# A gated recurrent layer: weights loaded by quarters of 32 rows, and two small moves inside a step

## The chip, the cores and the metric

The kernel runs on one core of a Trainium2 chip. The metric is the device time of one execution in microseconds (us); before the change it is 1395.19 us, the median of three runs (1394.82 to 1395.47). Every engine of the core has its own instruction queue and runs it in order: TensorE (PE; its weight loads are shown apart as PEld), VectorE (DVE), ScalarE (ACT), GpSimd (POOL) and SyncE (SP). SyncE only issues DMAs here; ScalarE and GpSimd issue a few as well.

## The reference

The input x has 64 sequences of 128 steps with 512 values each, h starts from `cond_1024`, and the result is x plus the states of a gated recurrent layer, all in float32:

```python
def step(h, inp):
    x_t, prop = inp
    comb = jnp.concatenate([x_t, h], axis=-1)
    z = jax.nn.sigmoid(comb @ Wz + bz)
    r = jax.nn.sigmoid(comb @ Wr + br)
    comb2 = jnp.concatenate([x_t, r * h], axis=-1)
    h_cand = jnp.tanh(comb2 @ Wh + bh)
    h_new = (1.0 - z) * h + z * h_cand
    h_next = jnp.where(prop, jnp.tanh(h_new @ Wp + bp), h_new)
    return (h_next, h_new)
```

Every fourth step is a prop step, in which a projection follows (31 of the 128). Wz, Wr and Wh are 1024 x 512: the upper 512 rows meet x, the lower 512 meet h. Wp is 512 x 512.

## The kernel before

**Layout.** A matrix of 512 x 512 lies in SBUF as `[128, K = 4, 512]`: four chunks k of 128 rows. The partitions are four quarters q of 32 (`part(q)`), and partition 32q + e of chunk k holds row q*128 + k*32 + e. The three upper halves lie in one tile `wx`, the lower halves in `wh[R]`, `wh[Z]`, `wh[H_]`, the projection in `wp`. A state h lies as 128 partitions x 256 values, in two halves `s_` of 128.

**The part that depends on x** is worked out ahead. For steps 0 to 3 and the last two by plain products (`plain`, `plain_last`), for all the others by a scheme of seven products instead of eight, for which sums of weight blocks are formed in place in `wx` (`sum_outer_1`, `sum_inner_1`). Chunks 0, 1 and 2 of `wx` are changed by that, chunk 3 isn't. All these products are units in a `queue`, and `fill(n)` puts n of them into TensorE's order at fixed places of a step: a list `PLACES` for the steady steps, `HEAD` and `TAIL` for the first and last ones. The results, with biases, become the seeds that `seed` copies into PSUM before a gate adds its part.

**A step** (the loop at L611) is, in program order: gate R on TensorE (16 matmul calls, 32 instructions); sigmoid of r, r*h and its transpose by halves; the seed of R for the next step; gate Z, its sigmoid, `keep` = (z - 1)*h; the seed of Z; in a prop step a copy of the projection's bias `bias_p` into PSUM (L695); `places[0]` units; gate H; its tanh by halves, each multiplied by z; one subtraction of `keep` over both halves (L727); the transpose to `hT`; the seed of H; `places[1]` units; in a prop step the projection with its tanh and transpose, and `places[2]` units. GpSimd adds h to x in `xr`, and SyncE stores four steps at a time.

**The start.** SyncE issues, in this order: half of the first x (ScalarE issues the other half), 12 DMAs for `wx` (R, Z, H; four chunks each), 4 for `wh[R]`, 8 for the next part of x, 4 for `wh[Z]`, 4 for `wh[H_]`, then x for steps 4 to 7 (`xr_1`) and 8 to 11 (`xs_2`), 4 for `wp` and 4 for `bias_p`. GpSimd issues the bias rows, waits for chunk 1 of R (`held`, L119) and then issues h0. TensorE runs 112 matmuls over zeros (`idle`) and then works in a fixed order: the x products of steps 0 and 1 for R, the spreading of the bias rows, the same products for Z and H, then step 0, in which 12 units stand between gate Z and gate H.

**The end.** In step T - 7 `reload` (L427) fetches chunks 2, 0 and 1 of `wx` again, since the last two steps use the plain weights. `plain_last` has the products of chunk 3 first, then chunks 2, 0, 1 for step T - 2, gate by gate, and then those of step T - 1. The SyncE queue then loads the last `xr`.

Of the kernel before, what the change touches and what calls it, by code (L numbers as in the profile page):

```python
# [18 lines left out]
def kernel(  # L19
# [14 lines left out]
    nc = tc.nc  # L34
    B, T, D = x.shape
    H = h0.shape[1]
    P = 128
    S = 2
    V = B // S
    NQ = P // V  # L40
    J = H // NQ
    C = 2
    K = D // P
# [4 lines left out]
    R, Z, H_ = range(3)  # L48
# [22 lines left out]
    wx = const.tile([P, K, 3, H], F32, name="wx")  # L71
    wh = [const.tile([P, K, H], F32, name=f"wh_{i}") for i in range(3)]
    wp = const.tile([P, K, H], F32, name="wp")
# [3 lines left out]
    gates_in = (Wr, Wz, Wh)  # L77
# [5 lines left out]
    def part(q):  # L83
        return slice(q * V, (q + 1) * V)

    def load_x(tile_, t0, n, j=0, engs=(nc.sync,)):
        i = 0
        for h in range(S):
            for q in range(NQ):
                engs[i % len(engs)].dma_start(  # L90
                    out=tile_[part(q), j : j + n, h, :], in_=x[ts(h, V), t0 : t0 + n, ts(q, J)]
                )
                i += 1

    def load_w(wt, w, k, eng=nc.sync):
        eng.dma_start(
            out=wt[:, k, :],
            in_=w.rearrange("(q k e) n -> k q e n", q=NQ, k=K)[k],
        )

    xr = {}

# [5 lines left out]
    bias_p = const.tile([P, S, J], F32, name="bias_p")  # L108
    new_xr(0)
    load_x(xr[0], 0, 2, engs=(nc.sync, nc.scalar))  # L110
    for i in range(3):
        for k in range(K):
            load_w(wx[:, :, i, :], gates_in[i][:D], k)

    for i, b in enumerate((br, bh, bz)):
        nc.gpsimd.dma_start(out=bias_row[:, i, :], in_=b.rearrange("(o n) -> o n", o=1))
# [3 lines left out]
    for h in range(S):  # L120
        nc.gpsimd.dma_start(
            out=h_init[:, h, :],
            in_=h0[ts(h, V), :].rearrange("b (q j) -> q b j", q=NQ),
        )
    for i in range(3):
        for k in range(K):
            load_w(wh[i], gates_in[i][D:], k)
        if i == 0:
            load_x(xr[0], 2, 2, 2)

# [5 lines left out]
    def load_xs(g):  # L136
        if g * Q4 < T:
            xs[g] = one.tile([P, Q4, S, J], F32, tag=f"xs{g % 2}", name=f"xs_{g}")
            load_x(xs[g], g * Q4, Q4)
# [1 line left out]
    new_xr(1)  # L141
    load_x(xr[1], Q4, Q4)
    load_xs(2)
    for k in range(K):
        load_w(wp, Wp, k)
    for q in range(NQ):
        nc.sync.dma_start(
            out=bias_p[part(q)],
            in_=bp.rearrange("(o d c j) -> c o d j", o=1, d=2, c=2)[q % 2].broadcast_to(
                [V, S, J]  # L150
            ),
# [3 lines left out]
    P_ = 3  # L155
    r, z = rec[H_][:, 1], rec[Z][:, 1]

    def gate_ps(i):
        return rec[0][:, 1] if i == P_ else rec[i][:, 0]
# [66 lines left out]
    def crossed(dst, h, ps, func):  # L226
        for d in range(2):
            nc.scalar.activation(  # L228
                dst[ts(d, 2 * V), h, :], ps[ts(h, 2 * V), d, :], func
            )  # L230

    def turn(dst, src):
        nc.vector.transpose(out=dst, in_=src)  # L233
# [134 lines left out]
    def seed(i, t):  # L368
        if t < T:
            nc.scalar.copy(  # L370
                gate_ps(i).rearrange("p d (c n) -> p d c n", c=C),
                G[t][:, :, :, i, :].rearrange("p c d n -> p d c n"),
            )
# [51 lines left out]
        return seq  # L425

    def reload():  # L427
        for k in (2, 0, 1):
            for i in range(3):
                load_w(wx[:, :, i, :], gates_in[i][:D], k)  # L430

    MB = {}

# [177 lines left out]
    for t in range(T):  # L611
        g, j = divmod(t, Q4)
        prop = j == CHUNK - 1 and t < T - 1
# [60 lines left out]
            turn(rhT[:, s_, :], rh[:, s_, :])  # L674
        if t != 3:
            seed(R, t + 1)
        if last:
            seed(H_, t)
        join(0)
# [2 lines left out]
        keep = two.tile([P, S, J], F32, tag="keep", name=f"keep_{t}")  # L682
        for s_ in range(S):
            crossed(z, s_, gate_ps(Z), AF.Sigmoid)
        nc.vector.scalar_tensor_tensor(  # L685
            out=keep, in0=z, scalar=1.0, in1=h, op0=ALU.subtract, op1=ALU.mult
# [4 lines left out]
        if t == 3:  # L691
            seed(R, t + 1)
        seed(Z, t + 1)
        if prop:
            nc.scalar.copy(gate_ps(P_), bias_p)  # L695
        if last:
            nc.gpsimd.tensor_sub(xr[g][:, j], xr[g][:, j], keep)
        if t == 0:
# [8 lines left out]
        if t == T - 7:  # L707
            reload()

        gate(H_, rhT, wh[H_])  # L710
        h_new = two.tile([P, S, J], F32, tag="h", name=f"h_{t}")
        hT = None if last else new_T("hT", f"hT_{t}")
        cand = two.tile([P, S, J], F32, tag="c", name=f"c_{t}")
        for s_ in range(S):
            crossed(cand, s_, gate_ps(H_), AF.Tanh)
            c = z[:, s_, :]
            nc.vector.tensor_mul(c, cand[:, s_, :], c)  # L717
            if last:
                o = xr[g][:, j, s_, :]
                nc.vector.tensor_add(o, c, o)  # L720
                (nc.sync, nc.scalar)[s_].dma_start(
                    out=out[ts(s_, V), t, :].rearrange("b (q n) -> q b n", q=NQ),
                    in_=o,
                )
                continue
        if not last:
            nc.vector.tensor_sub(h_new, z, keep)  # L727
            turn(hT, h_new)
        if t < T - 2:
            seed(H_, t + 1)  # L730
# [64 lines left out]
        n = 0  # L795
        if t >= T - CHUNK:
            n = 3 if t == T - 2 else 0
        elif j == Q4 - 1:
            n = 4
        if n:  # L800
            for s_ in range(S):
                for q in range(NQ):
                    nc.sync.dma_start(
                        out=out[ts(s_, V), t - n + 1 : t + 1, ts(q, J)],
                        in_=xr[g][part(q), j - n + 1 : j + 1, s_, :],
# [50 lines left out]
```

## Time and profile before

| | |
|---|---|
| median of the runs | 1395.19 us |
| profiled execution | 1394.77 us |
| its span, first to last instruction | 1392.7 us |
| mean granted clock of TensorE | 0.983 |
| TensorE matmul busy | 1324.7 us (95%) |
| VectorE busy | 733.7 us (53%) |
| ScalarE busy | 728.3 us (52%) |
| GpSimd busy | 887.4 us (64%) |
| TensorE busy, 0 to 128 us | 96.1 us |
| TensorE busy, 128 to 1320 us | 1170.5 of 1192 us |
| TensorE busy, 1320 to 1392.7 us | 58.1 us |

A page of the profile gives each engine's busy time, its busy share in 40 slices of the span (a digit is tenths, 9 is 90% or more), the clock that TensorE was granted (PEclk, tenths of full speed) and the mean busy share of the core's 16 DMA engines. A timeline row is: start, duration, engine, line, operation, output<-input, shapes, count, and in brackets how long the engine had been idle before and what released it. L202 is the matmul helper of all gates and units; the tile names tell them apart. L228 is the activation helper, L370 the seed, L717 the product with z. SPq, ACTq and PEq are an engine's queue: a DMA row there is the issue of the DMA, not its transfer.

### The profile page before, as it was taken

To read this page: it belongs to the slowest core of one execution; us is meant where nothing else is said; L and a number is where in the kernel's file an instruction comes from. 1 tells how busy PE (TensorE), PEld (TensorE's weight loads), DVE (VectorE), ACT (ScalarE), POOL (GpSimd) and SP (SyncE) were. 2 spreads that over 40 slices of the span, in tenths; PEclk is the share of its full clock that TensorE was granted. 3 is DMA by queue.
4 is the path that set the end of the run, shared out by engine and by line. 5 is a ranking of instruction groups with operands and counts; after the bars stand their busy time and mean duration, and the time that the engine had idled before them with its cause. 6 is when DMAs were issued, how large, how long until landed. Compare 5 with 4: busy or idle time off the path is not lost. (4 is left out here: it accounts for less than half of the span.)

```text
span 1392.7 us, 59942 instructions
## 1 busy us (share of the span) xinstructions
PE 1324.7 (95%) x26024; PEld 924.6 (66%) x26024; DVE 733.7 (53%) x1909; ACT 728.3 (52%) x2401; POOL 887.4 (64%) x1030
## 2 busy tenths in 40 slices
PE   7599999999999999999999999999999999999987
PEld 2256766767676676766667677676767667676654
DVE  0254555555555555555555555555555555555533
ACT  0034555555555555555555555555555555555544
POOL 1277776767777676767757676775767667576420
PEclk7699999999999999999999999999999999999999
DMA  2330111112101111110111111011111111111030
GB/s 97 109 93 21 41 48 37 48 33 54 42 21 48 46 48 33 48 44 23 48 48 48 33 42 45 27 48 49 48 33 33 48 32 48 47 35 33 18 100 17
DMA packets 114148, 63.14 MB, mean 45 GB/s; under 512 B 12604, under 2 KB 109116, under 8 KB 113884
## 3 DMA queue, kind: packets, MB, share of 16 engines
q1 hardware_dynamic: 113176, 58.97, 15.1%
q8 instruction: 204, 3.34, 1.0%
q14 instruction: 60, 0.49, 0.1%
q10 hardware_dynamic: 452, 0.20, 0.1%
q0 software_dynamic: 256, 0.14, 0.0%
HBM read 42.47 MB, written 16.78 MB: 43 GB/s over the span
## 5 line engine op out<-in xcount | busy, mean ns | idle before, releaser
L228 ACT ACTIVATE rec_h<-rec_r 64x128 f32<-64x128 f32 x512 | 128.0, 250 | 347.7 <-PE rec_r L202 291.8
L202 PE MATMUL rec_h<-wh,rhT 128*32 128x256 f32 x4096 | 274.4, 381 | 5.4 <-DVE rh L673 3.7
L202 PEld LDWEIGHTS rec_h<-wh,rhT 128*32 128x32 f32 x4096 | 166.0, 110 | 76.7 <-DVE rh L673 24.7
L202 PE MATMUL rec_r<-wh,hT 128*32 128x256 f32 x3072 | 184.9, 381 | 12.6 <-DVE hT L233 11.6
L202 PE MATMUL rec_z<-wh,hT 128*32 128x256 f32 x3072 | 183.8, 379 | 0.0
L793 POOL TENSOR_TENSOR xr<-xr,h 128x256 f32<-128x256 f32 x127 | 93.1, 733 | 133.7 <-DVE h L727 133.7
L228 ACT ACTIVATE c<-rec_h 64x128 f32<-64x128 f32 x512 | 139.5, 272 | 71.4 <-PE rec_h L202 64.8
L527 POOL TENSOR_TENSOR cp<-mb,mb 128x768 f32<-128x768 f32 x75 | 137.1, 1828 | 42.5 <-DVE mb L496 38.9
L527 POOL TENSOR_TENSOR mb<-mb,mb 128x768 f32<-128x768 f32 x58 | 106.2, 1831 | 83.0 <-DVE mb L496 83.0
L202 PEld LDWEIGHTS rec_r<-wh,hT 128*32 128x32 f32 x3072 | 96.6, 110 | 85.2 <-DVE hT L233 24.7
L673 DVE TENSOR_TENSOR rh<-rec_h,h 128x128 f32<-128x128 f32 x192 | 56.0, 291 | 173.0 <-ACT rec_h L228 173.0
L717 DVE TENSOR_TENSOR rec_z<-c,rec_z 128x128 f32<-128x128 f32 x256 | 75.7, 296 | 131.4 <-ACT c L228 126.3
L202 PEld LDWEIGHTS rec_z<-wh,hT 128*32 128x32 f32 x3072 | 103.8, 110 | 62.0
L228 ACT ACTIVATE rec_z<-rec_z 64x128 f32<-64x128 f32 x512 | 128.0, 250 | 26.9 <-PE rec_z L202 11.8
L527 POOL TENSOR_TENSOR cp<-mb 128x768 f32<-128x768 f32 x47 | 86.1, 1832 | 60.7 <-ACT rec_h L370 59.2
L469 ACT COPY cq<-scratch_q 128x384 f32<-128x384 f32 (+1 forms) x214 | 102.4, 479 | 22.0 <-PE scratch_q L202 18.3
L532 POOL TENSOR_TENSOR mb<-mb,bias_x 128x768 f32<-128x768 f32 x35 | 64.2, 1834 | 43.9 <-DVE mb L496 43.9
L233 DVE STREAM_TRANSPOSE rhT<-rh 128x128 f32<-128x128 f32 x256 | 79.8, 312 | 8.7
L492 DVE TENSOR_TENSOR mb<-scratch_q,cx 128x384 f32<-128x384 f32 (+1 forms) x107 | 58.1, 543 | 49.1 <-ACT cq L469 49.1
L685 DVE SCALAR_TENSOR_TENSOR keep<-rec_z,h 128x256 f32<-128x256 f32 x96 | 40.8, 425 | 79.0 <-ACT rec_z L228 79.0
L370 ACT COPY rec_z<-cp 128x256 f32<-128x256 f32 x128 | 48.2, 376 | 61.9 <-DVE keep L685 61.9
L527 POOL TENSOR_TENSOR cp<-cp,mb 128x768 f32<-128x768 f32 x29 | 53.2, 1834 | 32.7 <-DVE mb L496 31.6
(157 smaller groups left out, 2817.2 us busy)
## 6 DMA issues: line engine op xcount, KB each, us to landing
out_dram<-xr SPq DMA_DIRECT2D x249, 64.0 KB
xr<-in_x_dram SPq DMA_DIRECT2D x248, 64.0 KB
xs<-in_x_dram SPq DMA_DIRECT2D x240, 64.0 KB
wx<-in_L_cond_Wr_dram SPq DMA_DIRECT2D x7, 256.0 KB
wx<-in_L_cond_Wz_dram SPq DMA_DIRECT2D x7, 256.0 KB
wx<-in_L_cond_Wh_dram SPq DMA_DIRECT2D x7, 256.0 KB
wh<-in_L_cond_Wr_dram SPq DMA_DIRECT2D x4, 256.0 KB
wh<-in_L_cond_Wz_dram SPq DMA_DIRECT2D x4, 256.0 KB
```

The lines of the kernel that those rows point to most:

```text
L202: nc.tensor.matmul(ps[part(2 * h + c)], lhsT=lhs(h), rhs=rhs(c), start=start, stop=True, skip_group_check=True,)
L228: nc.scalar.activation(dst[ts(d, 2 * V), h, :], ps[ts(h, 2 * V), d, :], func)
L233: nc.vector.transpose(out=dst, in_=src)
L370: nc.scalar.copy(gate_ps(i).rearrange("p d (c n) -> p d c n", c=C), G[t][:, :, :, i, :].rearrange("p c d n -> p d c n"),)
L469: nc.scalar.copy(c[:, :nm], ps[:, :nm])
L492: nc.vector.tensor_add(blocks(1, 1), runs(q_ps[:, :nm]), runs(T2[what][:, :nm]))
L527: nc.gpsimd.tensor_add(dst, a, b)
L532: nc.gpsimd.tensor_add(m, m, v.unsqueeze(1).to_broadcast([P, 2, 3 * J]))
L673: nc.vector.tensor_mul(rh[:, s_, :], r[:, s_, :], h[:, s_, :])
L685: nc.vector.scalar_tensor_tensor(out=keep, in0=z, scalar=1.0, in1=h, op0=ALU.subtract, op1=ALU.mult)
L717: nc.vector.tensor_mul(c, cand[:, s_, :], c)
L793: nc.gpsimd.tensor_add(xr[g][:, j], xr[g][:, j], h_new)
```

## The change

Four edits. `load_w` no longer issues one DMA for each chunk of 128 rows (source cut into q, e, n) but one for each quarter of 32 partitions, with chunks k0 to k1 in it (source cut into e, k, n), over one queue or several in turn. R's part of `wx` goes in two pairs of chunks, the quarters in turn on SyncE and ScalarE; every other matrix goes as four DMAs on SyncE. `reload` goes matrix by matrix, chunks 0 to 2 in each DMA: 12 DMAs where there were 9. The copy of `bias_p` moves from behind the seed of Z to behind the seed of R (in step 3, where that seed comes later, to the same place without it). The subtraction of `keep` goes into the loop over the halves, so that half 0 is done between the two products with z.

```diff
-    def load_w(wt, w, k, eng=nc.sync):
-        eng.dma_start(
-            out=wt[:, k, :],
-            in_=w.rearrange("(q k e) n -> k q e n", q=NQ, k=K)[k],
-        )
+    def load_w(wt, w, k0=0, k1=K, engs=(nc.sync,)):
+        for q in range(NQ):
+            engs[q % len(engs)].dma_start(
+                out=wt[part(q), k0:k1, :],
+                in_=w[q * P + k0 * V : q * P + k1 * V, :].rearrange("(k e) n -> e k n", e=V),
+            )
...
-    for i in range(3):
-        for k in range(K):
-            load_w(wx[:, :, i, :], gates_in[i][:D], k)
+    for k in range(0, K, 2):
+        load_w(wx[:, :, R, :], gates_in[R][:D], k, k + 2, (nc.sync, nc.scalar))
+    for i in (Z, H_):
+        load_w(wx[:, :, i, :], gates_in[i][:D])
...
-        for k in range(K):
-            load_w(wh[i], gates_in[i][D:], k)
+        load_w(wh[i], gates_in[i][D:])
...
-    for k in range(K):
-        load_w(wp, Wp, k)
+    load_w(wp, Wp)
...
     def reload():
-        for k in (2, 0, 1):
-            for i in range(3):
-                load_w(wx[:, :, i, :], gates_in[i][:D], k)
+        for i in range(3):
+            load_w(wx[:, :, i, :], gates_in[i][:D], 0, 3)
...
         if t != 3:
             seed(R, t + 1)
+        if prop:
+            nc.scalar.copy(gate_ps(P_), bias_p)
         if last:
             seed(H_, t)
         join(0)
...
         seed(Z, t + 1)
-        if prop:
-            nc.scalar.copy(gate_ps(P_), bias_p)
...
                 continue
+            nc.vector.tensor_sub(h_new[:, s_, :], c, keep[:, s_, :])
         if not last:
-            nc.vector.tensor_sub(h_new, z, keep)
             turn(hT, h_new)
```

## The prediction

> **What bounds the kernel now.** I read the page's slices first, then SyncE's own timeline, then the stretches, and last the instruction timeline at the places the change touches. The slices:
>
> ```profile
> PE   7599999999999999999999999999999999999987
> PEclk7699999999999999999999999999999999999999
> DMA  2330111112101111110111111011111111111030
> ```
>
> One slice is 34.8 us. From the third on TensorE is the bound: between 128 and 1320 us it is busy for 1170.5 of 1192 us. What is not bound by it is the start (two slices of low clock, high DMA share) and the end. SyncE's queue shows what the start is made of:
>
> ```profile
> 5.54 10.47 SPq L96 DMA_DIRECT2D wx<-in_L_cond_Wz_dram  x4
> 16.06 10.02 SPq L96 DMA_DIRECT2D wx<-in_L_cond_Wh_dram  x4
> ...
> 50.39 9.71 SPq L96 DMA_DIRECT2D wh<-in_L_cond_Wh_dram  x4
> ...
> 176.88 3.65 SPq L90 DMA_DIRECT2D xr<-in_x_dram  x8
> ```
>
> Four weight DMAs (1.05 MB) hold the queue for 10 us; eight loads of x (0.52 MB) issue in 3.65 us. The columns of the next view are length, five busy times, the clock, the share of 16 DMA engines and GB/s:
>
> ```profile
> 18.00:20.00 2.00, 2.00 (x16) 0.39 (x12) 0.00 (x0) 0.00 (x0) 0.00 (x0) 0.50 0.26 102
> 142.00:143.00 1.00, 0.67 (x15) 0.42 (x16) 1.00 (x3) 0.00 (x0) 1.00 (x2) 1.00 0.54 155
> 1342.00:1343.00 1.00, 1.00 (x27) 0.73 (x20) 0.00 (x0) 0.00 (x0) 0.00 (x0) 1.00 0.60 198
> ```
>
> A weight stream by chunks of 128 rows runs at 102 GB/s with a share of 0.26, which is 4.2 of 16 engines; its source is cut into q, e, n with q = 4 outermost. The loads of x go to 32 partitions with 32 rows outermost, move in smaller runs (512 B), and still reach 0.54 and 155 GB/s. The new weight DMAs have the shape of the loads of x: 32 rows outermost. I read the 0.26 as four engines at work, and expect the new DMAs to use all 16.
>
> **Weights at the start.** TensorE waits for each chunk; the last waits are those that set the end of the start:
>
> ```profile
> 60.95 0.20 PEld L202 LDWEIGHTS rec_z<-wh,hT_init 128*32 128x32 f32 x8 [2.36 <-DMA wh<-in_L_cond_Wz_dram]
> ...
> 71.82 0.16 PEld L202 LDWEIGHTS rec_h<-wh,rhT 128*32 128x32 f32 x8 [1.58 <-DMA wh<-in_L_cond_Wh_dram]
> 72.06 0.78 PEld L202 LDWEIGHTS scratch_a<-wx,xT 128*32 128x32 f32 x16
> ```
>
> After 72.06 no matmul waits for a weight DMA until the end of the kernel, so the time at which the H gate of step 0 is done is what to compare. Up to the last chunk of Wz's lower half, 5.64 MB have moved (wx 3.15, h0 0.13, x's second part 0.26, wh for R and Z 2.10). At 102 GB/s this is 55.3 us; 60.95 leaves 5.65 us for the first x, the issue and the landing, which I keep.
>
> The rate after the change lies between 102 GB/s (nothing gained) and 16 engines at what one gives now, 102 / (0.26 x 16) = 24.5, so 392. The nearest rows are the loads of x: 155, which SyncE's issue held down (64 KB in 3.65 / 8 = 0.46 us is 144 GB/s), and 198, where the tail of a weight stream and loads of x ran together. I take 198, the most that a row shows with 32-row destinations in the stream. SyncE issues an unobstructed 256 KB weight DMA in 0.55 us, so issue doesn't limit at this rate.
>
> The Trainium skill, page "SBUF — State Buffer", section "Door 1: The DMA port swizzle", speaks against this edit: bandwidth follows how many of 16 ports the partitions reach, 32 partitions reach 8, and its advice is 128 partitions for every DMA-bound transfer. It gives 189 GB/s for 32 partitions against 328 for 128. The trace has 102 for 128 partitions and 155 for 32 of them, the other way round, so the rule alone would give a loss here; its figure of 189 would make the sum below 2.0 us worse (1.4 at the start, 0.6 in the reload).
>
> At 198, Wz lands at 5.65 + 28.5 = 34.1. Then, in TensorE's order, come gate Z (32 instructions), 12 fill units (96) and gate H (32). Rates: 54 ns an instruction at full clock (32 in 1.73 us, 77.45 to 79.18), 107 ns at half. Before 34.1 TensorE idles some 5 us, so I let it start at half clock, and let it rise after 5 us of work, as it did from 61.4 to 66.2: 47 instructions in 5.0, 81 in 4.4, so 43.5; wh for H landed at 39.4; gate H 1.7, so 45.2. The same working on the old trace gives 69.2 for the end of the fill, where the timeline has 69.25. The first fill unit behind gate H moves from 72.3 to 45.2: **-27.1**. VectorE does not take the place: from the keep of step 0 it has 7.5 us of work (63.2 to 70.7: `sum_outer`, three bias adds), so it is free near 46.4 and h about 1 us late, while 12 fill units (5.2 us) cover it. GpSimd's sums come forward with the weights. With the other ends: 392 GB/s leaves TensorE as the bound from 8.87 on, 192 + 32 + 32 + 96 + 32 instructions of 54 ns plus 1.4 for the bias rows, so 31.0 (-41.2); 155 gives 42.0 and so -19.2; 102 means the four chunks of a gate are worked off together after the last (+1.3).
>
> R's halves go out on SyncE and ScalarE. ScalarE gets four DMAs of about 0.5 us in front of a table load at 2.67; its first real work is at 20.75, so this is nothing; without that cover, 2 us. The bias rows, the `held` copy and h0 behind it stay on GpSimd's queue and come no later.
>
> **The reload.** Before, it went by chunk in the order 2, 0, 1, as the last readers finished:
>
> ```profile
> 1322.94 0.58 SPq L96 DMA_DIRECT2D wx<-in_L_cond_Wr_dram  x1
> ...
> 1327.65 0.83 PE L202 MATMUL scratch_r<-wx,s12r 128*32 128x192 f32 x16
> ...
> 1341.60 1.93 PE L202 MATMUL rec_r<-wh,hT 128*32 128x256 f32 x32 [0.94 <-DVE hT L233]
> ```
>
> Now each DMA carries all three chunks, so the first must wait for the readers of chunk 1 in the row at 1327.65, some 5.3 us later, and R, Z and H come one after another. 2.36 MB at 198 GB/s are 11.9 us; with 2.4 from issue to first byte and landing (first bytes of the reload lie 1.3 after its issue; 1.1 is my estimate for the landing, from chunks that a wait released 1.1 us after the stretches count their bytes) H lands near 1342.8. R and Z are in time (readers at 1338.42 and 1338.85). The reader of H at 1339.28 isn't: it and the unit behind it end at 1343.7, and behind them gate R of the next step waits, which started at 1341.60 after 0.94 us of wait for h. **+2.1**, and the steps after it are a chain, so it stays. 155 GB/s: H at 1346.1, +5.4. 392: the issue of 12 DMAs sets it, 0. 102: +13.3. Queued behind it on SyncE is the last load of x, used 20 us later.
>
> **h in halves.** The chain of one step:
>
> ```profile
> 1339.57 0.30 DVE L717 TENSOR_TENSOR rec_z<-c,rec_z 128x128 f32<-128x128 f32 x1 [1.29 <-ACT c L228]
> 1340.15 0.30 DVE L717 TENSOR_TENSOR rec_z<-c,rec_z 128x128 f32<-128x128 f32 x1 [0.29 <-ACT c L228]
> 1340.55 0.42 DVE L727 TENSOR_TENSOR h<-rec_z,keep 128x256 f32<-128x256 f32 x1
> 1341.01 0.45 DVE L233 STREAM_TRANSPOSE hT<-h 128x256 f32<-128x256 f32 x1
> ```
>
> First product to transpose: 1.44. After: product 0.40 (start to start, 1340.15 to 1340.55), half a subtraction 0.25 to 0.33 (0.29 for such a tile at L673), product 0.40, half 0.33: 1.38 to 1.46. The first half blocks the second product for about what the smaller last one saves. Only where TensorE waits for hT (63 times, 30 us) can it gain, at most 63 x 0.07 = 4.4. Where VectorE runs late anyhow (61 products out of 254 did not wait for a tanh, so at most 30 steps), the extra instruction costs 0.18: 5.4. I take **0**. The added 127 x 0.16 = 20 us lie in VectorE's 47% of idle time.
>
> **The bias of the projection.**
>
> ```profile
> 691.71 0.37 ACT L695 COPY rec_r<-bias_p 128x256 f32<-128x256 f32 x1
> 692.10 1.14 ACT L228 ACTIVATE c<-rec_h 64x128 f32<-64x128 f32 x4
> ```
>
> The tanh starts straight behind it. In the new place, behind the seed of r, it stands before the sigmoid of z, which also follows its predecessor without a gap (689.42 + 0.38, then 689.82): sigmoid, keep and seed of z come 0.38 later, and the tanh finds the same time. **0**; bounds: -2.2 (gate H was done 0.07 before the tanh, 31 times) and +11.8 (all 31 x 0.38 on the path).
>
> **Sum.** 1394.77 (this execution; span 1392.7 and 2.1 around it) - 27.1 + 2.1 = 1369.8. The median of the runs is 0.4 above it: **1370**.
>
> **Rivals.** *More than eight ports' worth* (over 300 GB/s): TensorE bounds the start, 1395.2 - 41.2 = 1354. For it: 24.5 GB/s an engine. Against: no row is above 198. Chance 0.10. *The rate of x* (155 and less): 1395.2 - 19.2 + 5.4 = 1381. For it: the stretch at 142; against: its issue limit. 0.13. *The weights stay slow* (slower side): the 32-row DMAs give no more than 102 GB/s, each gate starts only at its last quarter, and the reload stalls the tail: 1395.2 + 1.3 + 13.3 = 1410. It decides below some 122 GB/s, where start (-9.2) and reload (+9.2) cancel. For it: 128 rows fill every partition at once, 32 rows a quarter; against: 155 with smaller runs. 0.10, and 0.03 for a rate near that balance, no change. The forecast has 0.64.
>
> Its own range is 1366 to 1374. The 8 in 10 take in most of both neighbours on the faster side: 1355 to 1384. About 0.2% (2.8 us) is what a measurement here can tell from nothing. Faster 0.87, same 0.03, slower 0.10.
>
> **What would show it.** Right: weight stretches near 200 GB/s with a share above 0.5; full clock from about 40 us; a wait of TensorE of 2 to 4 us for wx near the reload; half subtractions before the second product at no gain. Wrong: a share of 0.26 still, matmuls of gate Z waiting past 50 us, or ScalarE's sigmoid of z late enough in the prop steps that TensorE waits for h there.

## The result, and the profile after

The changed kernel takes 1372.93 us, the median of four runs (1372.32 to 1374.43), beside 1395.30 before: a ratio of 0.9842, with a 95% interval of 0.9825 to 0.9859. The forecast was 1370, in a range of 1355 to 1384. The profiled execution took 1372.32, with a span of 1370.3 against 1392.7. The slices of the changed kernel:

```profile
PEclk9999999999999999999999999999999999999999
DMA  8401112101111111112101111111111101111030
```

The clock of the first two slices, 7 and 6 tenths before, is now 9, and the DMA engines have a high share (8 tenths) in the first slice alone. SyncE's queue and two stretches of the changed kernel:

```profile
6.19 2.53 SPq L97 DMA_DIRECT2D wx<-in_L_cond_Wz_dram  x4
11.45 5.99 SPq L97 DMA_DIRECT2D wh<-in_L_cond_Wr_dram  x4
18.27 8.06 SPq L90 DMA_DIRECT2D xr<-in_x_dram  x8
26.38 1.86 SPq L97 DMA_DIRECT2D wh<-in_L_cond_Wz_dram  x4
```

```profile
18.00:20.00 2.00, 2.00 (x24) 1.15 (x20) 0.00 (x0) 0.00 (x0) 0.00 (x0) 0.50 1.06 227
24.00:26.00 2.00, 2.00 (x40) 0.96 (x31) 1.09 (x3) 0.38 (x1) 1.96 (x2) 1.00 0.30 70
```

In the first of these stretches the weight stream runs at 227 GB/s and all 16 engines are busy (1.06, with overlapping packets), where it was 102 and 0.26. The stretches of 2 us between 4 and 24 us have 172 to 266. But there is a hole: from 18.3 to 26.3 us eight loads of x of 32 KB hold SyncE, the engines run low behind them (70 GB/s), and Wz's lower half is issued only then. TensorE's timeline:

```profile
33.48 3.64 PE L202 MATMUL rec_z<-wh,hT_init 128*32 128x256 f32 x32 [5.41 <-DMA wh<-in_L_cond_Wz_dram]
...
44.19 1.05 PE L202 MATMUL scratch_a<-wx,xT 128*32 128x256 f32 x16
```

The first fill unit behind gate H of step 0 starts at 44.19, where it was 72.27: 28.1 us earlier. Only 22.4 of them are left at the end of the span. Setting the transposes of h in both traces side by side, step by step, shows where the rest goes: 28.1 us ahead in steps 1 and 2, 28.3 in step 10, 26.7 in step 37, 24.8 in step 79, 22.5 in step 121, 22.4 in step 126. It is lost evenly over the whole run, and not at random: about 0.10 in each prop step, 0.18 in each step t = 5 mod 8, next to nothing elsewhere.

### The profile page after: what moved, and what is told of

It reads as the page before. It is cut to its first block, busy times and chain, and to the rows that moved or that the text cites. A ratio compares the mean times of both kernels' runs of the same rounds, so it can differ in the third digit from the quotient of the medians.

```text
span 1370.3 us, 60091 instructions
## 1 busy us (share of the span) xinstructions
PE 1315.0 (96%) x26024; PEld 925.3 (68%) x26024; DVE 753.5 (55%) x2036; ACT 730.2 (53%) x2401; POOL 887.3 (65%) x1030
## 5 line engine op out<-in xcount | busy, mean ns | idle before, releaser
L202 PE MATMUL rec_r<-wh,hT 128*32 128x256 f32 x3072 | 184.9, 381 | 14.4 <-DVE hT L233 13.3
L725 DVE TENSOR_TENSOR h<-rec_z,keep 128x128 f32<-128x128 f32 x254 | 74.0, 292 | 16.4
```

The source lines that it names most:

```text
L202: nc.tensor.matmul(ps[part(2 * h + c)], lhsT=lhs(h), rhs=rhs(c), start=start, stop=True, skip_group_check=True,)
L725: nc.vector.tensor_sub(h_new[:, s_, :], c, keep[:, s_, :])
```

## The experiments

All times are medians; ratios are to the kernel before, run beside them on the same chip, with 95% intervals. The start itself differs from run to run: in five runs with the same loads at the start (the changed kernel and four kernels below), gate Z of step 0 began between 31.9 and 34.5 us. Differences of a microsecond or two are therefore read from the steps, not from the medians.

### What the two small moves cost

The subtraction over both halves again, the rest as changed:

```diff
-            nc.vector.tensor_sub(h_new[:, s_, :], c, keep[:, s_, :])
         if not last:
+            nc.vector.tensor_sub(h_new, z, keep)
             turn(hT, h_new)
```

> The changed kernel with the subtraction of keep over both halves again, all else as changed. Theory A (the two small moves gave back what is missing after the start): the first of every eight-step period's late steps, t = 5 mod 8, loses 0.18 us no more (15 times), so about 2.7 us faster than the changed kernel, near 1370.2. Rival B (the moves are neutral, and the 5.7 us between step 6 and the end come from a shifted meeting of stores, loads and GpSimd's sums): 1372.9.

Measured: 1368.64 us (1367.76 to 1369.49), ratio 0.9806 (0.9792 to 0.9819), 4.3 under the changed kernel. Step by step, it moves ahead of the changed kernel by 0.18 in each step t = 5 mod 8 and by 0.01 to 0.02 in most others; 3.6 us from step 4 to step 122, where theory A expected 2.7.

The bias copy behind the seed of z again, the rest as changed:

```diff
             seed(R, t + 1)
-        if prop:
-            nc.scalar.copy(gate_ps(P_), bias_p)
...
         seed(Z, t + 1)
+        if prop:
+            nc.scalar.copy(gate_ps(P_), bias_p)
```

> The changed kernel with the projection's bias copied behind the seed of z again. Theory A: each of 31 prop steps is 0.10 us shorter, so about 3.1 us faster than the changed kernel, near 1369.8. Rival B: 1372.9. Rival C (the half subtraction alone is the loss, also in the prop steps): 1372.9 here and 1367 without the halves.

Measured: 1369.69 us (1368.83 to 1370.25), ratio 0.9813 (0.9800 to 0.9826), 3.2 under the changed kernel; it gains 0.10 us in each prop step and nothing in the others, 3.1 us from step 7 to step 121.

Both undone, so that only the loads are changed:

> Only the new weight loads: subtraction and bias copy as in the kernel before. Theory A: both losses gone, about 5.8 us under the changed kernel, near 1367, 28 us under the kernel before. Rival B: 1372.9.

Measured: 1366.59 us (1366.21 to 1366.82), ratio 0.9791 (0.9778 to 0.9804). Its lead over the kernel before is 28.4 us in step 5 and 29.0 in step 122: nothing is given back on the way. Against the changed kernel it gains 6.4 us in these steps, close to the 3.6 and 3.1 of the two runs above together.

Only the two moves, with the loads of before:

> Only the half subtractions and the moved bias copy, weights loaded by chunks of 128 rows as before. Theory A: about 5.8 us slower than the kernel before, near 1401. Rival B: 1395.3, no change. If the halves saved anything by themselves: below 1395.

Measured: 1400.57 us (1400.37 to 1402.95), ratio 1.0042 (1.0028 to 1.0056); its lag behind the kernel before grows from nothing to 5.7 us with the same pattern of steps. Theory A holds in all four runs and rival B falls: it does not need the earlier start. Rival C falls with the run in which the bias alone was put back.

Why each costs is in the rows. VectorE of the kernel before, in a step t = 5 mod 8:

```profile
714.40 0.55 DVE L496 TENSOR_TENSOR mb<-scratch_y,cq 128x384 f32<-128x384 f32 x1
714.87 0.69 DVE L717 TENSOR_TENSOR rec_z<-c,rec_z 128x128 f32<-128x128 f32 x2
715.66 0.42 DVE L727 TENSOR_TENSOR h<-rec_z,keep 128x256 f32<-128x256 f32 x1
716.12 0.45 DVE L233 STREAM_TRANSPOSE hT<-h 128x256 f32<-128x256 f32 x1
```

The same step of the changed kernel:

```profile
688.99 0.28 DVE L716 TENSOR_TENSOR rec_z<-c,rec_z 128x128 f32<-128x128 f32 x1
689.38 0.29 DVE L725 TENSOR_TENSOR h<-rec_z,keep 128x128 f32<-128x128 f32 x1
689.78 0.30 DVE L716 TENSOR_TENSOR rec_z<-c,rec_z 128x128 f32<-128x128 f32 x1
690.11 0.29 DVE L725 TENSOR_TENSOR h<-rec_z,keep 128x128 f32<-128x128 f32 x1
690.43 0.45 DVE L233 STREAM_TRANSPOSE hT<-h 128x256 f32<-128x256 f32 x1
```

No row has an idle time: VectorE comes late from evacuating a batch, and both tanhs are done by then. There is nothing left to overlap with, so the fourth instruction is simply added: from the first product to the transpose it is 1.44 us where it was 1.25. In a step where VectorE does wait for a tanh, the same distance is 1.45 (1326.04 to 1327.49 in the changed kernel) where it was 1.44 (1339.57 to 1341.01): the split gains nothing there either.

ScalarE of the changed kernel, in a prop step:

```profile
663.44 0.38 ACT L370 COPY rec_r<-cp 128x256 f32<-128x256 f32 x1
663.85 0.38 ACT L677 COPY rec_r<-bias_p 128x256 f32<-128x256 f32 x1
664.25 1.09 ACT L228 ACTIVATE rec_z<-rec_z 64x128 f32<-64x128 f32 x4
665.83 0.38 ACT L370 COPY rec_z<-cp 128x256 f32<-128x256 f32 x1 [0.49 <-DVE keep L686]
666.22 1.14 ACT L228 ACTIVATE c<-rec_h 64x128 f32<-64x128 f32 x4
```

The copy stands on one chain with the tanh in either place, but its price isn't the same: behind the seed of r it starts 0.41 after it, behind the seed of z it started 0.31 after it (691.40, 691.71), and what follows comes 0.39 to 0.40 later in both. From the seed of r to the tanh it is 2.78, where it was 2.68 (689.42 to 692.10). Why the two copies stand further apart here was not tried; that both go to one PSUM tile (`rec_r`) and the seed of z to another is a guess.

### A place where the copy costs nothing

In the rows above ScalarE waits 0.49 us for the keep, between the sigmoid and the seed of z. The run with the loads only, with the copy there:

```diff
             crossed(z, s_, gate_ps(Z), AF.Sigmoid)
+        if prop:
+            nc.scalar.copy(gate_ps(P_), bias_p)
```

> Loads only, and the projection's bias copied between the sigmoid of z and the seed of Z, where ScalarE waits 0.49 us for the keep in every step. The copy takes 0.37. Theory S (the copy cost time in both places because ScalarE had no gap there; in a gap it costs nothing): the tanh of a prop step starts when gate H is done, 0.07 us earlier than with the copy behind the seed of Z, 31 times, so 2.2 us under the run with the loads only, near 1364.4. Rival (a copy into that bank costs wherever it stands): 1366.6 or more.

Measured: 1365.73 us (1363.36 to 1368.05), ratio 0.9790 (0.9777 to 0.9803). By the median it can't be told from the run with the loads only. By the steps it can: 0.08 us gained in each prop step and nothing elsewhere, 2.2 us from step 4 to step 121, on top of a profiled start that happened to be 1.7 later and a reload that cost 2.1 more (its rows follow under the reload below).

### What makes the weight loads fast

Chunks in order again, but each as four DMAs of 32 rows, 64 KB; small moves undone:

```diff
+        for k in range(k0, k1):
             for q in range(NQ):
                 engs[q % len(engs)].dma_start(
-                    out=wt[part(q), k0:k1, :],
-                    in_=w[q * P + k0 * V : q * P + k1 * V, :].rearrange("(k e) n -> e k n", e=V),
+                    out=wt[part(q), k, :],
+                    in_=w[q * P + k * V : q * P + (k + 1) * V, :],
                 )
```

> Small moves undone; weights by chunk k again, but each chunk as four DMAs of 32 rows (64 KB, one 2 KB row to a partition) instead of one of 128 rows. Theory E (the outermost count of a DMA decides how many of the 16 engines work; 32 gives all): share above 0.5 in the weight stream, and the rate is held by the issue, 64 KB in some 0.46 us or 140 GB/s; Wz's lower half lands near 45 us instead of 33.5, the reload (36 DMAs, 16 us) stalls the end some more: 1378 to 1386. Rival F (a DMA is fast because four rows go to each partition): 102 GB/s and a share of 0.26, time of the kernel before or more.

Measured: 1387.99 us (1383.65 to 1389.20), ratio 0.9943 (0.9923 to 0.9962), 2 us above the expected range. Gate Z of step 0 had its last chunk at 45.13 us, as expected; the reload cost 7.5 us. The same DMAs with the source cut with 4 outermost:

```diff
-                    in_=w[q * P + k * V : q * P + (k + 1) * V, :],
+                    in_=w[q * P + k * V : q * P + (k + 1) * V, :].rearrange("(e a) n -> a e n", a=4),
```

> As the run by chunks of 32 rows, but the source of each DMA is cut so that 4 is its outermost count (rows 0, 4, 8 ... first). The rows land in another order in their quarter, so the output isn't the reference's; bytes, DMAs, partitions and queues are the same. Theory E: four engines again, a share of 0.26 and 102 GB/s, Wz's lower half lands near 60 us, and with the reload that must wait: 1395 to 1410. Rival G (32 partitions or the quarter order is what makes it fast): the same time as the run by chunks of 32 rows.

Measured: 1412.98 us (1412.57 to 1414.34), ratio 1.0129 (1.0114 to 1.0144): 18.3 us behind the kernel before in the last steps, 3.6 to 4.4 of them from the start and 14.7 from the reload. A stretch of the weight stream in each of the two, the shorter cut first:

```profile
16.00:20.00 4.00, 2.91 (x52) 1.63 (x48) 0.75 (x2) 0.71 (x2) 0.75 (x1) 1.00 0.53 143
```

```profile
20.00:24.00 4.00, 3.76 (x32) 0.95 (x24) 0.00 (x0) 1.02 (x3) 0.99 (x1) 0.50 0.27 102
```

The first is at its issue limit (64 KB in 0.46 us is 143 GB/s), the second at four engines' pace. Bytes, number, partitions and queues of the DMAs are the same, only the outermost count of the source differs: theory E holds, F and G fall. The Trainium skill states such a rule, page "DMA: Bandwidth & Descriptors", section "Why a DMA increments its semaphore by 16 and not by 1": the number of engines is the largest number up to 16 that divides the outermost dimension of both sides. With 4 of 16 it gives a share of 0.25, where the rows have 0.26 and 0.27; with 32 it gives 16, where the changed kernel has 1.06.

Row p*4 + k in partition p, so that a matrix is one DMA with 128 partitions outermost, and the transposes read with a step:

```diff
+            out=wt[:, k0:k1, :],
+            in_=w.rearrange("(p k) n -> p k n", k=K)[:, k0:k1, :],
...
-        in_=src[:, i].rearrange("p h (k e) -> p h k e", k=K),
+        in_=src[:, i].rearrange("p h (e k) -> p h k e", k=K),
...
-        nc.vector.transpose(out=dst, in_=src)
+                in_=src.rearrange("p (e k) -> p k e", k=K),
```

> Small moves undone; row p*4 + k of a matrix in partition p, chunk k, so that each matrix is one DMA with 128 partitions outermost; the transposes of x, h and r*h read their rows with a step of 4 to match. Theory P: over 300 GB/s, the start bound by TensorE, 1352 to 1360 if a transpose with a step costs what it cost (0.31, 0.45 us). If the step doubles a transpose: 0.3 to 0.5 us a step on the chain of h, 1385 to 1420.

Measured: 1385.29 us (1384.91 to 1387.39), ratio 0.9928 (0.9912 to 0.9945), 18.7 over the run with the loads only. The rate came as theory P had it, and the time at the lower edge of the second range: a transpose with a step took 1.4 to 1.5 times as long, not twice. The weight stream and the dearer transposes of this run:

```profile
8.00:12.00 4.00, 4.00 (x80) 2.08 (x76) 0.00 (x0) 0.00 (x0) 0.75 (x2) 1.00 1.05 403
```

```profile
703.30 0.67 DVE L238 STREAM_TRANSPOSE hT<-h 128x256 f32<-128x256 f32 x1
...
706.97 0.43 DVE L233 STREAM_TRANSPOSE rhT<-rh 128x128 f32<-128x128 f32 x1
```

403 GB/s, 7.7 us more gained by step 1; but 0.67 and 0.43 us for transposes that took 0.45 and 0.31, and they stand on the chain of h: 28 us given back over the steps. So 32 partitions do cost something. GB/s divided by share x 16 is what an engine moves in its busy time, and the stretches shown give all four pairings:

| | four engines | sixteen engines |
|---|---|---|
| into 128 partitions | 102 / (0.26 x 16) = 24.5 | 403 / (1.05 x 16) = 24.0 |
| into 32 partitions | 102 / (0.27 x 16) = 23.6 | 227 / (1.06 x 16) = 13.4 |

Neither sixteen engines nor 32 partitions alone slow an engine down; the two together do. This fits the port rule that the prediction weighed (8 ports against 16, 218 and 436 GB/s by its page). It isn't shown to be the cause: the DMAs behind the 403 are also larger, 0.5 to 1.05 MB against 0.26, and 218 isn't a limit here, since 32-row DMAs went over it in the start and further in the reload (below). The kernel before could not show any of this, since its 128 partitions were written by four engines.

Quarters 0 and 1 on SyncE, 2 and 3 on ScalarE at the same time:

```diff
-            engs[q % len(engs)].dma_start(
+            engs[q // 2 * (len(engs) - 1)].dma_start(
...
-        load_w(wx[:, :, i, :], gates_in[i][:D])
+        load_w(wx[:, :, i, :], gates_in[i][:D], engs=(nc.sync, nc.scalar))
-        load_w(wh[i], gates_in[i][D:])
+        load_w(wh[i], gates_in[i][D:], engs=(nc.sync, nc.scalar))
```

> Small moves undone; quarters 0 and 1 of wx and wh issued by SyncE, 2 and 3 by ScalarE at the same time. Theory P (32 partitions take a share of the ports into SBUF, so that 16 engines stall at 225 GB/s; quarters from both halves of the partitions in flight lift this): over 300 GB/s in the weight stream, gate Z of step 0 starts near 24 instead of 33.5 us, and the time is 5 to 11 us under the run with the loads only, near 1359. Rival (the rule that two such DMAs serialize): at most 2 us under it. Rival (ScalarE blocked by a full queue): slower than it.

Measured: 1367.56 us (1366.46 to 1369.50), ratio 0.9803 (0.9789 to 0.9818), no gain. Two things cancel: the stream reaches 306 GB/s between 16 and 20 us (239 to 269 in the three stretches of 4 us before it), so two such DMAs do not simply serialize there; but ScalarE, busy issuing until 24.5, copies the bias rows only at 26.05, and TensorE waits 6.3 us for them. The rate passed theory P's 300 in that one stretch alone, and since two queues and both halves of the partitions come together here, which of them lifts it isn't shown. The time has the cause that the rival with the blocked ScalarE names; that the run is slower for it is not clear of the noise.

### The hole in the stream, and the best version

The eight loads of x behind Wz's lower half instead of in front of it:

```diff
-        if i == 0:
+        if i == 1:
             load_x(xr[0], 2, 2, 2)
```

> Loads only, small moves undone, and the eight loads of x for steps 2 and 3 issued behind Wz's lower half instead of in front of it. In the run with the loads only those eight hold SyncE from 16.8 to 25.1 us, and the DMA engines fall to 55 GB/s between 24 and 26. Theory H (the small loads stand in the way of Wz, by their issue and not by their bytes): gate Z of step 0 starts 3 to 5 us earlier than at 31.9, TensorE has hardly a gap before it and keeps full clock, so 5 to 8 us less in all, near 1360. Rival (they only change places: x late now, and VectorE's join of x stands in front of the keep): 1366.6, no change, or more. Bytes alone (0.26 MB at 225 GB/s): 1.2 us less.

Measured: 1362.55 us (1362.02 to 1363.22), ratio 0.9763 (0.9749 to 0.9776), 4.0 under the run with the loads only. The stretch from 24 to 26 us has 227 GB/s where it had 55, and gate Z begins at 29.95 instead of 31.90. TensorE waits 1.85 us before it instead of 5.06 and keeps its clock (32 instructions in 1.93 us instead of 3.64), as theory H had it; only the start moved 1.9 us and not 3 to 5. More than the bytes' 1.2 us, less than theory H's 5 to 8: the loads of x now hold SyncE from 22.2 to 30.7, in front of Wh, and the hole is now between 30 and 32 us, at 55 GB/s. Why eight small loads take about 1 us each to issue there was not tried.

Then also wx by whole DMAs of 128 partitions (R's two pairs and the reload as well), with the step only in the transposes of x, which aren't on the chain of h:

```diff
+    def load_whole(wt, w, k0=0, k1=K):
+        nc.sync.dma_start(
+            out=wt[:, k0:k1, :],
+            in_=w.rearrange("(p k) n -> p k n", k=K)[:, k0:k1, :],
+        )
...
-        load_w(wx[:, :, i, :], gates_in[i][:D])
+        load_whole(wx[:, :, i, :], gates_in[i][:D])
...
-        in_=src[:, i].rearrange("p h (k e) -> p h k e", k=K),
+        in_=src[:, i].rearrange("p h (e k) -> p h k e", k=K),
```

> As x_behind_wz, and wx with row p*4 + k in partition p as DMAs of 128 partitions, only the transposes of x with a step of 4; wh, h and r*h by quarters as before. At 400 GB/s wx lands near 13 us, gate R starts near 20.5, gate Z near 23: 3 to 5 us under x_behind_wz at the start. Steps: transposes of x 0.43 to 0.66 us, 128 of them, off the chain of h; if hidden, near 1356; if they make VectorE late as the extra subtraction did (0.18 us in one step of eight and more), up to 1364.

Measured: 1359.00 us (1357.46 to 1360.13), ratio 0.9738 (0.9725 to 0.9751). 4.8 us ahead of the run above in step 5 and still 4.5 in step 122: the dearer transposes of x are hidden. Gate R began at 22.62 and gate Z at 25.69 us, 2 to 3 later than expected. Last, the bias copy in ScalarE's gap on top:

> The run wx_whole with the bias copy in that gap: 2.2 us under it, near 1357. If the copy costs in the gap too: 1359 or more.

Measured: 1355.24 us (1354.16 to 1356.07), ratio 0.9717 (0.9703 to 0.9730); 2.8 us are gained from step 5 to step 121. ScalarE in a prop step of this run:

```profile
732.76 1.09 ACT L234 ACTIVATE rec_z<-rec_z 64x128 f32<-64x128 f32 x4
733.88 0.38 ACT L691 COPY rec_r<-bias_p 128x256 f32<-128x256 f32 x1
734.35 0.38 ACT L376 COPY rec_z<-cp 128x256 f32<-128x256 f32 x1
734.97 1.13 ACT L234 ACTIVATE c<-rec_h 64x128 f32<-64x128 f32 x4 [0.24 <-PE rec_h L208]
```

The seed of Z no longer waits for the keep, and the tanh waits for TensorE, not for ScalarE. This is the fastest version found, 17.7 us under the changed kernel and 39.1 under the kernel before that ran beside it.

## Why the prediction was right, and where it was not

**The sum, 1370 forecast, 1372.93 measured.** That it lies so near is in part luck. The start gained 1.0 us more than forecast and the reload cost 2.0 less, and against that stand some 5.8 us that were lost on the way from the two moves taken at nothing.

**What bounds the kernel, and the engines.** Right: 0.26 was four engines, and 32 rows outermost bring 16 (shown by the two runs that differ in that cut alone).

**The start, -27.1 forecast, -28.1 measured.** Right in size, with two errors in it that cancelled. The rate was 227 for much of the stream and not 198 GB/s, which by the prediction's sum would have landed Wz at 30.5; and the hole behind the eight loads of x put it back to 33.48 (34.1 forecast). The kernel before has such a hole too, in SyncE's queue and in a stretch of its start:

```profile
36.70 11.13 SPq L90 DMA_DIRECT2D xr<-in_x_dram  x8
```

```profile
48.00:50.00 2.00, 0.63 (x8) 0.00 (x0) 0.60 (x2) 0.82 (x4) 0.00 (x0) 0.50 0.14 36
```

The prediction named SyncE's queue, but priced x there by its bytes alone, so that the old hole lies unnamed in the 5.65 us that it kept for the first x, the issue and the landing. The clock went much as assumed: gate Z at half clock (32 instructions in 3.64 us), full from about 37.7, after 4.2 us of work where 5 were taken. VectorE's `sum_outer` stayed under the fill units.

**The port rule.** The row held against it compared 128 partitions on four engines with 32 on sixteen. It showed rightly that this change would gain, but not that the rule fails: with 16 engines on either side, 128 partitions took 403 GB/s and 32 took 227.

**The reload, +2.1 forecast, 0.1 measured.** Mis-sized is the time until H has landed: 14.3 us from the first issue (2.4 and 11.9) in the sum, 12.0 in the changed kernel (1305.72 to 1317.74). The wait moved to the readers of chunk 1, as forecast, and TensorE did wait for H, in the changed kernel's rows:

```profile
1317.74 0.64 PE L202 MATMUL scratch_r<-wx,xT 128*32 128x256 f32 x8 [0.44 <-DMA xr<-in_x_dram]
...
1319.12 1.93 PE L202 MATMUL rec_r<-wh,hT 128*32 128x256 f32 x32 [0.30 <-DVE hT L233]
```

Here the stream ran at 242 to 315 GB/s for most of its time, so the wait was 0.44, and the next gate R still waited 0.30 for h: next to nothing reached the end. (The releaser that the row names is a load of x; the unit reads wx.) But this is one execution. Five other profiled runs whose reload is issued in the same way lost 0.2 to 0.6 us there (with the loads only 13.1 us to the landing, a wait of 1.56, and 0.6 lost), and the run with the copy in the gap lost 2.7:

```profile
1312.45 0.64 PE L202 MATMUL scratch_r<-wx,xT 128*32 128x256 f32 x8 [2.08 <-DMA wx<-in_L_cond_Wh_dram]
...
1313.31 3.62 PE L202 MATMUL rec_r<-wh,hT 128*32 128x256 f32 x32
```

There H landed 13.7 us after the first issue, the stream ran at 200 to 248 GB/s between 1303 and 1311 us, and behind the wait gate R ran at half clock (0.50 granted from 1314 to 1316 us, 3.62 us for what took 1.93). So the wait and its path were right, and the forecast lies within what the same reload cost from one execution to another; why its rate differs was not tried. The two runs with wx whole, whose reload goes in DMAs of 128 partitions, lost nothing there.

**h in halves, 0 forecast, some 3.6 measured.** The step that failed is "I take 0". Its two bounds were the right mechanisms, the distance of 1.38 to 1.46 and 0.18 in a late step; 1.45 was measured for the first, so there was no gain to set against the second. 15 steps at 0.18 are 2.7, the rest is 0.01 to 0.02 in others.

**The bias copy, 0 forecast, 3.1 measured.** The step that failed is that the tanh finds the same time: the chain was right, but the copy was taken at one price in both places. The row in front of it, the seed, has to be read too: 0.41 behind the one, 0.31 behind the other.

**The rivals.** A rate of over 300 GB/s at the start came with all partitions in one DMA, and for 4 us with both halves in flight. DMAs of 64 KB, the size of the loads of x at 142 us, stood at 143 GB/s with the issue as the limit, as argued for x. The slower side, 1410 if the 32-row DMAs gave 102 GB/s, was built with a cut by 4: 1412.98, with 14.7 us from the reload where 13.3 were forecast.

## What to carry to other kernels

Read the DMA engines' share beside the GB/s: a stream at a quarter of the engines was mended here by another outermost dimension. The instruction that was split to overlap cost its whole 0.18 us in every step where its engine already ran late, so look for the steps without a wait before splitting. The copy that must stand on ScalarE's chain cost nothing in a wait of that engine; elsewhere it cost 0.08 or 0.18 us a prop step, and not its whole 0.37, since TensorE would have been the next to wait for.

## What was not expected of the hardware

With all 16 engines busy, DMAs into 32 partitions on one queue ran at 227 GB/s at the start, at 242 to 315 for most of the changed kernel's reload, and at 200 to 248 in the same reload of the run with the copy in the gap. The reload's DMAs carry three chunks instead of four in both, so that alone doesn't make the difference; what does was not tried. A VectorE transpose of 32 x 32 blocks that reads with a step of 4 values takes 0.67 instead of 0.45 us (256 values) and 0.43 instead of 0.31 (128). Eight loads of 32 KB behind a full stream of weights held SyncE for 8 us and left the engines at 55 to 79 GB/s for 2 to 4 us.
